# Moving the first group's DMA traffic between issuing queues, and two routers by half a product, in a Winograd-form adapter FFN

## The chip, the core and the metric

The kernel runs on one core of a Trainium2 chip. The core has a matrix engine (PE, TensorE), a vector engine (DVE, VectorE), a scalar engine (ACT, ScalarE), a general engine (POOL, GpSimd) and a synchronization engine (SP, SyncE). PE, DVE, ACT and POOL compute; SP, ACT and POOL also issue DMAs, each from its own in-order instruction queue, and all DMAs run on the same 16 DMA engines. The metric is the device time of one execution in microseconds, the median of several runs; lower is better.

## The reference, cut to what matters

```python
W = weights[condition]                        # 64 samples, each a 64x64 matrix
y = einsum('bct,bcd->bdt', x, W)              # x: 64 x 64 x 1024
xf = y.reshape(-1, 1024)                      # 4096 rows
scores = xf @ Wr.T                            # Wr: 64 x 1024
top_vals, top_idx = top_k(scores, 16)
gates = softmax(top_vals)                     # scattered into G, 4096 x 64
h = einsum('nd,krd->nkr', xf, A)              # A: 64 x 16 x 1024
out = einsum('nkr,kdr->nd', h * G[:, :, None], B)   # B: 64 x 1024 x 16
return x + out * 2.0
```

So there are two products of a 4096 x 1024 matrix with a 1024 x 1024 matrix (A and B), a small matrix per sample, and a router that scales the middle result by 64 gates per row. All arithmetic is in fp32.

## The kernel before, in words

The 4096 rows are worked in eight groups of 512 rows (`g` from 0 to 7; "group 2" is `g = 1`, "group 8" is `g = 7`). The per-sample matrix is applied after the product with A and not before it: `z = x A` first (with the router's 64 columns appended, 16 to each block of 256), then `gated` multiplies by the gathered per-sample matrices on PE and by the gates on DVE, and writes the four quarters of h into the tiles `hb`. Then follows the product with B, and the residual x is added.

Both large products are written in the Strassen-Winograd form: seven products of half-size blocks in place of eight, with sums of blocks before and after. In groups 2 to 8 this is done on two levels, so that each of the seven products (a "parent") is itself made of seven small products ("leaves"). In group 1 there is one level only, with whole blocks of A or B (`whole_parent`), and beside it DVE makes the leaf operands that all later groups need: for each of the seven first-level blocks of A (kind `h`) and B (kind `o`), differences of its quarters (`leaf_steps`). Each is written to a staging tile `staged` from the pool `bsum` (four buffers, used in turn) and stored to a scratch tensor in DRAM (`leaf_d`). Leaves that are plain quarters of a block that was itself computed (`raw`, three per block, for the four blocks p5, p6, p7, p4 of B) are stored without a step on DVE. In the trace, `hs_p_p` and `os_p_p` are the staging tiles of A and B, `h_p_p` and `o_p_p` their scratch tensors, and `lh_p_p`, `lo_p_p` the leaves fetched back (`fetch`, L458) into a ring of 13 tiles.

The order of work is written by hand. Parents run in the order h of group 1, o of group 1, h of group 2, h of group 3, o of group 2, and so on. Each parent has four lists of hooks: "mid" (after its first half), "late", "end" (after its second half), and a call `at(n, when, f)` hangs `f` on parent `n`. A hook runs in program order on whatever engine and queue its instructions belong to. The instructions of one engine are not reordered: if DVE waits for a buffer, all that stands behind it on DVE waits too, and the same is true of the DMA queues of SP, ACT and POOL.

Names and lines that matter below:

- L110 to L124: the first loads. x block 00 and the small `cond_b` go through ACT's queue; the other x blocks, the blocks of A, `wr_sb` (router weights) and the blocks of B through SP's.
- L183: `st`, the router's score product of group 1 (x with `wr_sb`), between the second and third product.
- L417: the store of a staged leaf; L411: the three `raw` stores; SP issues both, ACT the stores of the first six leaves (`apart`).
- L90 and L87 are the helpers `sub` and `add` on DVE; every sum has one of these lines.
- L489 `prepare`: four DVE sums that make the left leaf operands `l_t` of the next parent; without them the third small product of that parent can't start. It is called in the middle of the parent before.
- `a_sums`, `b_sums`: the first-level block sums; `b_sums 4` makes the block b21 that the product p4 of B uses (L542 `o_w<-b,hb`).
- L542: PE products of group 1. L505: the small products of groups 2 to 8. L556, L598, L605: copies out of PSUM on ACT.
- L161: `gather`, four indirect DMAs on POOL for each group's per-sample matrices.
- The router of groups 2 to 8: `scores`, `route_top`, `exps` (ACT), `rest` (DVE, one call for each of four tiles), `scaled` (four ACT instructions, L292), `gates` (PE transposes and an ACT copy), `gated`. In groups 2 and 8 (`near`) these stand closer together, since the next parents are already the o parents that use them.
- L741: the store of a quarter of the output, on SP; L735: the load of the residual x.

Of the kernel before, what the change touches and what calls it, by code (L numbers as in the profile page):

```python
# [9 lines left out]
F32 = mybir.dt.float32  # L10
# [5 lines left out]
P = 128  # L16
BANK = 512
# [4 lines left out]
CH = 4  # L22
HN = TPG * P // 2
HALF = BANK // 2
# [5 lines left out]
def kernel(  # L30
# [26 lines left out]
    nc = tc.nc  # L57
# [4 lines left out]
    K = wr_t.shape[1]  # L62
    NT = N // P
    NG = NT // TPG
# [19 lines left out]
    epool = early.enter_context(tc.tile_pool(name="epool", bufs=1, side="right"))  # L84
# [4 lines left out]
    def sub(o, a, b):  # L89
        nc.vector.tensor_tensor(o, a, b, ALU.subtract)  # L90
# [4 lines left out]
    def load_x(g: int, i: int, j: int, queue=nc.sync, parts=1):  # L95

        t = xq[g, i, j] = xp.tile([P, CH, HN], F32, tag=f"x{i}{j}", name=f"x_{g}_{i}{j}")
        for k in range(parts):
            s = ts(k, CH // parts)
            queue.dma_start(t[:, s, :], x_t[g, i, j][:, s, :])  # L100

    def load_block(name, src, r, c, pool, parts=1):
        t = pool.tile(src.shape[2:], F32, name=name)
        for k in range(parts):
            s = ts(k, CH // parts)
            nc.sync.dma_start(t[:, s, :], src[r, c][:, s, :])
        return t

    cond_b = const.tile([P, B], I32)
    load_x(0, 0, 0, nc.scalar, 2)  # L110
    a11 = load_block("a11", a_t, 0, 0, apool, 4)
    nc.scalar.dma_start(cond_b, cond.to_broadcast([P, B]))
    load_x(0, 1, 0)
    a21 = load_block("a21", a_t, 1, 0, apool)
    load_x(0, 0, 1)
    load_x(0, 1, 1)
    a12 = load_block("a12", a_t, 0, 1, apool)
    wr_sb = epool.tile([P, 2 * CH, K], F32, name="wr_sb")
    nc.sync.dma_start(wr_sb, wr_t.rearrange("(c p) k -> p c k", p=P))
    a22 = load_block("a22", a_t, 1, 1, apool)  # L120
    b12 = load_block("b12", b_t, 0, 1, bpool)
    b22 = load_block("b22", b_t, 1, 1, bpool)
    b11 = load_block("b11", b_t, 0, 0, epool)
    b21 = load_block("b21", b_t, 1, 0, bpool)  # L124


    row_i = const.tile([P, 1], I32)
# [29 lines left out]
    def gather(g: int):  # L157
        w_st = small.tile([P, TPG, D], F32, tag="w_st", name=f"w_st_{g}")
        for i in range(TPG):
            n = g * TPG + i  # L160
            nc.gpsimd.indirect_dma_start(  # L161
                out=w_st[:, i, :],
                out_offset=None,
                in_=cw,
                in_offset=bass.IndirectOffsetOnAxis(ap=idx[:, n : n + 1], axis=0),
            )
# [206 lines left out]
    RAW = ("p1", "p2", "p3")  # L373
# [8 lines left out]
    WIDTH = {"h": HALF + KC, "o": HALF}  # L382

    def quads(t, w):

        return [[t[:, 2 * i : 2 * i + 2, ts(j, w)] for j in range(2)] for i in range(2)]

    leaf_d = {}
# [5 lines left out]
    for j, (r, c) in {"p1": (0, 0), "p2": (1, 0), "p3": (1, 1)}.items():  # L394
        (q11, _), (q21, q22) = quads(b_t[r, c], HALF)
        leaf_d.update({("o", j, "p1"): q11, ("o", j, "p2"): q21, ("o", j, "p3"): q22})

    def leaf_steps(k, j, block, apart=None):


        (q11, q12), (q21, q22) = quads(block, WIDTH[k])
        made = {}
        queue = nc.sync if apart is None else nc.scalar

        def staged(name):
            t = bsum.tile([P, 2 * (HALF + KC)], F32, tag="leaf", name=name)
            return t[:, : 2 * WIDTH[k]].rearrange("p (c k) -> p c k", c=2)

        def raw():
            for t, p in ((q11, "p1"), (q21, "p2"), (q22, "p3")):  # L410
                nc.sync.dma_start(leaf_d[k, j, p], t)  # L411

        def step(op_, p, a, b):
            def f():
                made[p] = staged(f"{k}s_{j}_{p}")
                op_(made[p], *(made[v] if isinstance(v, str) else v for v in (a, b)))
                queue.dma_start(leaf_d[k, j, p], made[p])  # L417

            return f

        if k == "o":
            steps = [
                step(sub, "p5", q12, q11),
                step(sub, "p6", q22, "p5"),
                step(sub, "p4", q21, "p6"),
                step(sub, "p7", q22, q12),
            ]
            return steps if j in RAW else [raw] + steps
        stay.update({(k, j, "p1"): q11, (k, j, "p2"): q21, (k, j, "p3"): q22, (k, j, "p5"): q12})
        t1 = q12 if apart is None else apart.rearrange("p (c k) -> p c k", c=2)  # L430
        steps = [
            step(sub, "p7", q22, q12),
            lambda: sub(t1, q12, q11),
            step(sub, "p6", q22, t1),
            step(sub, "p4", q21, "p6"),
        ]
        return steps if apart is None else steps + [lambda: nc.scalar.copy(q12, t1)]


    parents, to_fetch, ring, stay, fetched = [], [], [], {}, [0]  # L440
# [297 lines left out]
            )  # L738

    def store(st, i, j):  # L740
        nc.sync.dma_start(  # L741
            out[ds((st["g"] * TPG + 2 * i) * P, 2 * P), ts(j, BANK)].rearrange(
                "(s p) t -> p s t", p=P
            ),
            st["os"][i, j],
        )
# [71 lines left out]
    at3 = apool.tile([P, CH, 2 * (HALF + KC)], F32, name="at3")  # L818
    at4 = apool.tile([P, CH, 2 * (HALF + KC)], F32, name="at4")
    ar = {"p1": a11, "p2": a21, "p3": a22, "p4": at4, "p5": a12, "p6": at2, "p7": at3}  # L820
    bt2 = bpool.tile([P, CH, BANK], F32, name="bt2")
    bt3 = epool.tile([P, CH, BANK], F32, name="bt3")
    br = {"p1": b11, "p2": b21, "p3": b22, "p4": b21, "p5": b12, "p6": bt2, "p7": bt3}

    sts = [{"g": g} for g in range(NG)]
    for k, g in (
# [4 lines left out]
        st = sts[g]  # L831
# [20 lines left out]
    def sums(st, which, *steps):  # L852
        for s in steps:
            st[which][s]()
# [56 lines left out]
    st = sts[0]  # L911
    h, o = st["h"], st["o"]
    steps_of(first_steps["p1"], 4)
    rows_to_gather()
    gather(0)
    steps_of(first_steps["p2"], 4)
    x_operands(st)
    sums(st, "x_sums", "s1_s2")
    a_sums(1)
# [28 lines left out]
    for k, lst, n in (  # L948
        (h + 2, b_steps, 4),
        (h + 3, b_steps, 4),  # L950
        (h + 5, a_steps, 4),
        (h + 6, a_steps, 5),
        (o, a_steps, 2),
        (o + 1, b_steps, 5),
        (o + 1, a_steps, 1),
        (o + 2, a_steps, 6),
        (o + 3, a_steps, 2),
        (o + 4, b_steps, 7),
        (o + 5, b_steps, 7),
    ):  # L960
        at(k, "end", steps_of, lst, n)
    at(o + 6, "mid", steps_of, b_steps, 2)
    at(o + 6, "end", steps_of, b_steps, 99)
    at(h + 1, "mid", gather, 1)
    for i, j in ((0, 0), (1, 0), (0, 1), (1, 1)):
        at(o, "end", load_x, 1, i, j)
    at(o + 4, "end", second_level)
    at(o + 5, "mid", fetches, 3)
    at(o + 5, "end", fetches, 3)
    h = sts[1]["h"]  # L970
# [4 lines left out]

    for st in sts[1:]:
        n, g = st["h"] + 7, st["g"]
        near = g in (1, NG - 1)
        at(n + 1, "mid", scores, st)
        at(n + 1, "late", route_top, st)  # L980
        at(n + 2, "mid", exps, st, 0, 1)
        at(n + 2, "end", exps, st, 2, 3)
        if near:
            slots = ((2, "end"), (3, "late"), (3, "end"), (4, "late"))
            pairs = {
                1: (((5, "end"), (0, 0), (1, 1)), ((6, "mid"), (1, 0), (0, 1))),
                NG - 1: (((5, "end"), (0, 0), (1, 0)), ((7, "mid"), (1, 1), (0, 1))),
            }[g]
        else:
            slots = ((3, "end"), (5, "end"), (6, "end"), (7, "late"))  # L990
            pairs = (((8, "end"), (0, 0), (1, 0)), ((9, "mid"), (1, 1), (0, 1)))
        for i, (k, when) in enumerate(slots):
            at(n + k, when, rest, st, i)
        at(n + (4 if near else 8), "end" if near else "mid", scaled, st)
        at(n + (5 if near else 8), "mid" if near else "late", gates, st)
        for (k, when), *quarters in pairs:
            for i, j in quarters:
                at(n + k, when, gated, st, i, j)
# [3 lines left out]
    for st in sts:  # L1002
        g, h, o = st["g"], st["h"], st["o"]
# [72 lines left out]
```

## Time and profile before

| | us |
|---|---|
| median of 3 runs | 801.13 (800.57 to 802.12) |
| the profiled execution | 801.74 |
| its span in the profile | 799.7 |
| PE busy | 773.6 |
| DVE busy | 623.9 |
| POOL busy | 36.5 |
| mean granted TensorE clock | 0.991 of full speed |

The span is the time from the first to the last recorded instruction; 2.0 us of the execution lie around it. PE is busy for 97% of the span, so it is idle for 26.1 us. These are spread unequally: the page's second part cuts the span into 40 slices of 20 us, and the row PE shows less than "9" in the first two slices, in the seventh (120 to 140 us, "5"), and in the last. The seventh is also the only inner slice in which the row PEclk falls. The row DMA is high in the first two slices, low from 40 to 80 us, and high again from 80 us on.

How to read it: a row of the timeline gives start and duration in us, engine, line, operation, output and inputs, and in brackets how long the engine was idle before it and who released it. A matmul of group 1 is 128x512 and takes 0.43 us start to start; a parent of group 1 takes 6.9 us.

### The profile page before, as it was taken

What the parts mean: (1) busy time and instruction counts of PE and PEld (TensorE: products, weight loads), DVE (VectorE), ACT (ScalarE), POOL (GpSimd) and SP (SyncE); (2) the same over time, 40 slices, a digit from 0 to 9 for tenths busy, and PEclk for the clock granted to TensorE, in tenths of its full rate; (3) what the DMA queues carried; (4) which work ended last, traced back from release to release, by engine and by line L of the source; (5) the groups of instructions that cost most, each with busy time, mean ns of one, the idle gap of its engine ahead of it and who ended that gap; (6) DMA issues with size and microseconds to landing.
All of it is one profiled execution on the core that took longest, in us unless ns stands there. A gap on an engine that the chain in (4) does not pass through costs nothing.

```text
span 799.7 us, 14643 instructions
## 1 busy us (share of the span) xinstructions
PE 773.6 (97%) x5342; PEld 612.2 (77%) x5342; DVE 623.9 (78%) x1310; ACT 184.1 (23%) x490; POOL 36.5 (5%) x39
## 2 busy tenths in 40 slices
PE   8899995999999999999999999999999999999996
PEld 4444444888788888888888888888788888887885
DVE  2887575677888976888778977889768888688986
ACT  0230001222222222222222222222222231232221
POOL 2200200000020020000200002000100000000000
PEclk9999997999999999999999999999999999999998
DMA  8922779764879948889488977889588894687995
GB/s 326 400 109 99 257 255 372 255 213 119 301 219 291 333 132 310 282 271 343 140 315 274 304 246 251 273 282 322 166 302 251 279 351 124 223 263 243 355 379 203
DMA packets 114982, 208.49 MB, mean 261 GB/s; under 512 B 12256, under 2 KB 31456, under 8 KB 114016
## 3 DMA queue, kind: packets, MB, share of 16 engines
q1 hardware_dynamic: 112448, 204.02, 75.3%
q10 hardware_dynamic: 1440, 2.49, 0.8%
q0 software_dynamic: 1024, 1.05, 0.5%
q8 instruction: 43, 0.70, 0.3%
q14 instruction: 27, 0.22, 0.1%
HBM read 174.41 MB, written 33.11 MB: 260 GB/s over the span
## 4 chain that ended last, share of the span: by engine, by line
PE 89%; DMA 4%; DVE 4%; issue 2%; SPq 0%; ACT 0%; DVEq 0%; ACTq 0%
PE h_p_x L505 23%; PE o_p_x L505 20%; PE h_p_w L505 11%; PE o_p_w L505 10%; PE h_p_y L505 6%; PE o_p_y L505 5%; PE zp L324 4%; PE h_x L542 3%; DMA x<-in_x_t_dram 2%; PE h_w L542 2%; PE o_x L542 2%; PE o_w L542 1%; DVE o L87 1%; DMA o_p_p<-os_p_p 1%; DMA wr_sb<-in_wr_t_dram 1%
## 5 line engine op out<-in xcount | busy, mean ns | idle before, releaser
L505 PE MATMUL o_p_x<-lo_p_p,l_t 128*128 128x256 f32 x584 | 143.3, 379 | 1.9 <-ACT l_r L598 1.8
L505 PEld LDWEIGHTS o_p_x<-lo_p_p,l_t 128*128 128x128 f32 x584 | 110.9, 190 | 17.8 <-ACT l_r L598 2.2
L87 DVE TENSOR_TENSOR o<-o,m_o_p 128x1024 f32<-128x1024 f32 (+1 forms) x67 | 78.7, 1193 | 0.5
L87 DVE TENSOR_TENSOR m_h_p<-h_p_w,l_a 128x272 f32<-128x272 f32 x49 | 21.5, 439 | 62.9 <-PE h_p_w L505 62.9
L505 PE MATMUL h_p_x<-lh_p_p,l_t 128*128 128x272 f32 x196 | 54.1, 399 | 9.3 <-issue 8.8
L87 DVE TENSOR_TENSOR m_h_p<-m_h_p,m_h_p 128x1088 f32<-128x1088 f32 x49 | 62.3, 1283 | 0.2
L505 PE MATMUL h_p_x<-a,l_t 128*128 128x272 f32 x224 | 61.4, 397 | 0.0
L161 POOL DMA_INDIRECT w_st<-in_cw_dram,idx x32 | 35.7, 1116 | 543.8 <-PE zp L324 523.6
L505 PE MATMUL h_p_w<-lh_p_p,l_t 128*128 128x272 f32 x196 | 54.6, 402 | 0.0
L505 PEld LDWEIGHTS h_p_x<-lh_p_p,l_t 128*128 128x128 f32 x196 | 37.6, 193 | 17.7 <-issue 9.2
L505 PE MATMUL o_p_w<-lo_p_p,l_t 128*128 128x256 f32 x196 | 51.0, 383 | 0.0
L505 PEld LDWEIGHTS h_p_x<-a,l_t 128*128 128x128 f32 x224 | 43.1, 193 | 8.9
L337 DVE TENSOR_TENSOR hb<-zp,gg 128x512 f32<-128x512 f32 x64 | 40.0, 683 | 10.8 <-PE zp L324 10.8
L598 ACT COPY l_b<-h_p_x 128x272 f32<-128x272 f32 x49 | 18.9, 385 | 121.9 <-PE h_p_x L505 121.9
L505 PE MATMUL h_p_x<-at,l_t 128*128 128x272 f32 x168 | 45.4, 392 | 0.0
L505 PEld LDWEIGHTS h_p_w<-lh_p_p,l_t 128*128 128x128 f32 x196 | 37.1, 194 | 7.3
L598 ACT COPY l_b<-o_p_x 128x256 f32<-128x256 f32 x49 | 18.2, 372 | 103.2 <-PE o_p_x L505 103.2
L505 PEld LDWEIGHTS o_p_w<-lo_p_p,l_t 128*128 128x128 f32 x196 | 36.6, 190 | 5.1
L87 DVE TENSOR_TENSOR m_o_p<-o_p_w,l_a 128x256 f32<-128x256 f32 x48 | 20.3, 422 | 23.7 <-PE o_p_w L505 23.7
L324 PEld LDWEIGHTS zp<-w_st,m_h_p 64*64 64x64 f32 x2048 | 31.7, 135 | 8.4 <-issue 8.4
L505 PEld LDWEIGHTS h_p_x<-at,l_t 128*128 128x128 f32 x168 | 31.9, 190 | 6.6
L324 PE MATMUL zp<-w_st,m_h_p 64*64 64x64 f32 x2048 | 34.3, 220 | 0.8 <-issue 0.8
(162 smaller groups left out, 1329.6 us busy)
## 6 DMA issues: line engine op xcount, KB each, us to landing
lo_p_p<-o_p_p SPq DMA_DIRECT2D x280, 256.0 KB, 3.9
lh_p_p<-h_p_p SPq DMA_DIRECT2D x147, 272.0 KB, 5.5
o<-in_x_dram SPq DMA_DIRECT2D x32, 512.0 KB, 7.0
lo_p_p<-in_b_t_dram SPq DMA_DIRECT2D x63, 256.0 KB, 4.4
x<-in_x_t_dram SPq DMA_DIRECT2D x31, 512.0 KB, 5.0
out_dram<-o SPq DMA_DIRECT2D x31, 512.0 KB, 5.6
o_p_p<-os_p_p SPq DMA_DIRECT2D x28, 256.0 KB, 2.9
b<-in_b_t_dram SPq DMA_DIRECT2D x4, 1024.0 KB
```

Source lines behind the costliest of these rows:

```text
L87: nc.vector.tensor_tensor(o, a, b, ALU.add)
L161: nc.gpsimd.indirect_dma_start(out=w_st[:, i, :], out_offset=None, in_=cw, in_offset=bass.IndirectOffsetOnAxis(ap=idx[:, n : n + 1], axis=0),)
L324: nc.tensor.matmul(zp[b][e * D : (e + 1) * D, c, s, :], lhsT=halves(z)[r, s, c // 2, ds(c % 2 * P + e * D, D)], rhs=ws[g][r, 2 * i + s, :] ...
L337: nc.vector.tensor_tensor(tokens(hb[j, i])[:, :, :, b, :], zp[b], g_ij[:, :, :, b, :], ALU.mult)
L505: nc.tensor.matmul(bank, lhsT=v[:, c, :], rhs=w[:, c, :width], start=first and c == 0, stop=c == 1, skip_group_check=True,)
L542: nc.tensor.matmul(piles[n, s], lhsT=left()[j][:, c, ts(s, P)], rhs=w, start=c == 0 and PILES[kind][j].isupper(), stop=c == CH - 1, skip_g ...
L598: nc.scalar.copy(par["val"][n], par["bank"]["x"])
```

## The change

The edit moves DMA issues between queues, moves some of them in time, and moves hooks. No arithmetic is added or removed.

1. First loads: a11 comes in two parts and not four; x blocks 10 and 01 and `wr_sb` go through ACT's queue and not SP's; the four blocks of B are loaded only after the first leaf stores stand in SP's queue.
2. The first six leaves (`apart`) are stored through SP's queue and not ACT's, and four of them are staged in the four `hb` tiles, which are empty until the first `gated`.
3. All other leaf stores of A and B go through POOL's queue and not SP's. The `raw` stores leave the list of steps, go through POOL's queue too, and hang on parents of their own (`raw_leaves`), three of the four blocks earlier than before.
4. The stores of group 1's output quarters go through POOL's queue.
5. The four loads of group 2's x, which stood together behind the first o parent, are spread over the next four parents. The numbers of leaf steps for each parent change with the removed `raw` steps.
6. In groups 2 and 8, the second pair of `exps`, the four `rest`, `scaled`, `gates` and the first `gated` pair each stand half a product earlier. The other groups keep their places.

```diff
     load_x(0, 0, 0, nc.scalar, 2)
-    a11 = load_block("a11", a_t, 0, 0, apool, 4)
+    a11 = load_block("a11", a_t, 0, 0, apool, 2)
     nc.scalar.dma_start(cond_b, cond.to_broadcast([P, B]))
-    load_x(0, 1, 0)
+    load_x(0, 1, 0, nc.scalar)
     a21 = load_block("a21", a_t, 1, 0, apool)
-    load_x(0, 0, 1)
+    load_x(0, 0, 1, nc.scalar)
     load_x(0, 1, 1)
+    wr_sb = epool.tile([P, 2 * CH, K], F32, name="wr_sb")
+    nc.scalar.dma_start(wr_sb, wr_t.rearrange("(c p) k -> p c k", p=P))
     a12 = load_block("a12", a_t, 0, 1, apool)
-    wr_sb = epool.tile([P, 2 * CH, K], F32, name="wr_sb")
-    nc.sync.dma_start(wr_sb, wr_t.rearrange("(c p) k -> p c k", p=P))
     a22 = load_block("a22", a_t, 1, 1, apool)
-    b12 = load_block("b12", b_t, 0, 1, bpool)
...
@@ leaf_steps
+    unused = list(hb.values())
+
     def leaf_steps(k, j, block, apart=None):
...
-        queue = nc.sync if apart is None else nc.scalar
+        queue = nc.gpsimd if apart is None else nc.sync
         def staged(name):
+            if apart is not None and unused:
+                t = unused.pop().rearrange("p c k -> p (c k)")
+                return t[:, : 2 * WIDTH[k]].rearrange("p (c k) -> p c k", c=2)
             t = bsum.tile([P, 2 * (HALF + KC)], F32, tag="leaf", name=name)
...
-        def raw():
-            for t, p in ((q11, "p1"), (q21, "p2"), (q22, "p3")):
-                nc.sync.dma_start(leaf_d[k, j, p], t)
...
+    def raw_leaves(j, block):
+        (q11, _), (q21, q22) = quads(block, HALF)
+        for t, p in ((q11, "p1"), (q21, "p2"), (q22, "p3")):
+            nc.gpsimd.dma_start(leaf_d["o", j, p], t)
...
     def store(st, i, j):
-        nc.sync.dma_start(
+        (nc.sync if st["g"] else nc.gpsimd).dma_start(
...
     steps_of(first_steps["p2"], 4)
+    for t, r, c in ((b12, 0, 1), (b22, 1, 1), (b11, 0, 0), (b21, 1, 0)):
+        nc.sync.dma_start(t, b_t[r, c])
...
         (o, a_steps, 2),
-        (o + 1, b_steps, 5),
-        (o + 1, a_steps, 1),
-        (o + 2, a_steps, 6),
+        (o + 1, b_steps, 4),
+        (o + 1, a_steps, 2),
+        (o + 2, a_steps, 5),
         (o + 3, a_steps, 2),
-        (o + 4, b_steps, 7),
-        (o + 5, b_steps, 7),
+        (o + 4, b_steps, 6),
+        (o + 5, b_steps, 6),
...
-    for i, j in ((0, 0), (1, 0), (0, 1), (1, 1)):
-        at(o, "end", load_x, 1, i, j)
+    for k, (i, j) in enumerate(((0, 0), (1, 0), (0, 1), (1, 1))):
+        at(o + 1 + k, "mid", load_x, 1, i, j)
+    for n, when, j in ((h + 5, "mid", "p5"), (h + 6, "mid", "p6"), (o, "mid", "p7"), (o + 4, "mid", "p4")):
+        at(n, when, raw_leaves, j, br[j])
...
@@ router, groups 2 and 8 (the other groups as before)
-        at(n + 2, "end", exps, st, 2, 3)
+        at(n + 2, "mid" if g in (1, NG - 1) else "end", exps, st, 2, 3)
-            slots = ((2, "end"), (3, "late"), (3, "end"), (4, "late"))
-                1: (((5, "end"), (0, 0), (1, 1)), ((6, "mid"), (1, 0), (0, 1))),
-                NG - 1: (((5, "end"), (0, 0), (1, 0)), ((7, "mid"), (1, 1), (0, 1))),
+                ((2, "late"), (2, "end"), (3, "late"), (3, "end")),
+                (4, "mid"),
+                (4, "end"),
+                ((5, "mid"), (0, 0), (1, 1) if k == 1 else (1, 0)),
+                ((6, "mid"), (1, 0), (0, 1)) if k == 1 else ((7, "mid"), (1, 1), (0, 1)),
...
-        at(n + (4 if near else 8), "end" if near else "mid", scaled, st)
-        at(n + (5 if near else 8), "mid" if near else "late", gates, st)
+        at(n + scale[0], scale[1], scaled, st)
+        at(n + turned[0], turned[1], gates, st)
```

More of the change, by code (lines that the diff above doesn't have):

```diff
@@ L110 @@
     load_x(0, 0, 0, nc.scalar, 2)
-    a11 = load_block("a11", a_t, 0, 0, apool, 4)
+    a11 = load_block("a11", a_t, 0, 0, apool, 2)
     nc.scalar.dma_start(cond_b, cond.to_broadcast([P, B]))
-    load_x(0, 1, 0)
+    load_x(0, 1, 0, nc.scalar)
     a21 = load_block("a21", a_t, 1, 0, apool)
-    load_x(0, 0, 1)
+    load_x(0, 0, 1, nc.scalar)
     load_x(0, 1, 1)
+    wr_sb = epool.tile([P, 2 * CH, K], F32, name="wr_sb")
+    nc.scalar.dma_start(wr_sb, wr_t.rearrange("(c p) k -> p c k", p=P))
     a12 = load_block("a12", a_t, 0, 1, apool)
-    wr_sb = epool.tile([P, 2 * CH, K], F32, name="wr_sb")
-    nc.sync.dma_start(wr_sb, wr_t.rearrange("(c p) k -> p c k", p=P))
     a22 = load_block("a22", a_t, 1, 1, apool)
-    b12 = load_block("b12", b_t, 0, 1, bpool)
-    b22 = load_block("b22", b_t, 1, 1, bpool)
-    b11 = load_block("b11", b_t, 0, 0, epool)
-    b21 = load_block("b21", b_t, 1, 0, bpool)
     row_i = const.tile([P, 1], I32)
@@ L421, in leaf_steps @@
         if k == "o":
-            steps = [
+            return [
                 step(sub, "p5", q12, q11),
@@ L427, in leaf_steps @@
             ]
-            return steps if j in RAW else [raw] + steps
         stay.update({(k, j, "p1"): q11, (k, j, "p2"): q21, (k, j, "p3"): q22, (k, j, "p5"): q12})
@@ L820 @@
     ar = {"p1": a11, "p2": a21, "p3": a22, "p4": at4, "p5": a12, "p6": at2, "p7": at3}
+    b12, b22, b11, b21 = (
+        (epool if n == "b11" else bpool).tile([P, CH, BANK], F32, name=n)
+        for n in ("b12", "b22", "b11", "b21")
+    )
     bt2 = bpool.tile([P, CH, BANK], F32, name="bt2")
@@ L977 @@
         n, g = st["h"] + 7, st["g"]
-        near = g in (1, NG - 1)
         at(n + 1, "mid", scores, st)
@@ L981 @@
         at(n + 2, "mid", exps, st, 0, 1)
-        at(n + 2, "end", exps, st, 2, 3)
-        if near:
-            slots = ((2, "end"), (3, "late"), (3, "end"), (4, "late"))
-            pairs = {
-                1: (((5, "end"), (0, 0), (1, 1)), ((6, "mid"), (1, 0), (0, 1))),
-                NG - 1: (((5, "end"), (0, 0), (1, 0)), ((7, "mid"), (1, 1), (0, 1))),
[L988 to L991, printed above, removed]
+        at(n + 2, "mid" if g in (1, NG - 1) else "end", exps, st, 2, 3)
+        slots, scale, turned, *pairs = {
+            k: (
+                ((2, "late"), (2, "end"), (3, "late"), (3, "end")),
[3 more added lines that the diff above has]
+                ((6, "mid"), (1, 0), (0, 1)) if k == 1 else ((7, "mid"), (1, 1), (0, 1)),
+            )
+            for k in (1, NG - 1)
+        }.get(
+            g,
+            (
+                ((3, "end"), (5, "end"), (6, "end"), (7, "late")),
+                (8, "mid"),
+                (8, "late"),
+                ((8, "end"), (0, 0), (1, 0)),
+                ((9, "mid"), (1, 1), (0, 1)),
+            ),
+        )
         for i, (k, when) in enumerate(slots):
             at(n + k, when, rest, st, i)
-        at(n + (4 if near else 8), "end" if near else "mid", scaled, st)
-        at(n + (5 if near else 8), "mid" if near else "late", gates, st)
+        at(n + scale[0], scale[1], scaled, st)
+        at(n + turned[0], turned[1], gates, st)
         for (k, when), *quarters in pairs:
```

## The prediction, made before the changed kernel was run

> **What bounds the kernel now.** I read the page first: PE is busy 97% of the span, so only PE's gaps and PE's clock can give time back. Its slices show one inner hole, the seventh (120 to 140 us):
>
> ```profile
> PE   8899995999999999999999999999999999999996
> ...
> PEclk9999997999999999999999999999999999999998
> ```
>
> Then who PE waited for (total, times, longest in us), and PE's timeline around the hole:
>
> ```profile
> PE st L183 <- DMA wr_sb<-in_wr_t_dram: 2.7, 1, 2.7
> PE o_p_x L505 <- ACT l_r L598: 1.8, 1, 1.8
> ```
>
> ```profile
> 105.16 7.13 PE L542 MATMUL o_w<-b,hb 128*128 128x512 f32 x16 [1.07 <-DVE b L90]
> ...
> 129.83 2.15 PE L505 MATMUL h_p_x<-lh_p_p,l_t 128*128 128x272 f32 x4 [8.84 <-issue]
> 131.78 2.02 PE L505 MATMUL h_p_w<-lh_p_p,l_t 128*128 128x272 f32 x4
> ```
>
> One large gap, 8.84 us from 120.99, stands between group 1 and group 2; small ones are 2.7 (router weights), 1.07 (block b21), 1.83 (group 8, at 733.3) and 0.46 (group 2, at 210.9). After the large one PE is also slow: windows of 2 us show the clock at 1.00 until 124, 0.94 in 124 to 126, 0.50 from 126 to 136. So the clock fell about 4.7 us after PE stopped, and the sixteen small matmuls from 129.83 to 136.62 took 6.79 us where 4 x 0.92 = 3.67 is usual: 3.1 us more.
>
> Why the gap? The first leaf product of group 2 needs `l_t`, which DVE makes last in this queue:
>
> ```profile
> 92.55 0.69 DVE L90 TENSOR_TENSOR os_p_p<-bt 128x512 f32<-128x512 f32 x1 [9.06 <-DMA o_p_p<-os_p_p]
> ...
> 124.96 0.69 DVE L90 TENSOR_TENSOR os_p_p<-bt,os_p_p 128x512 f32<-128x512 f32 x1 [7.18 <-DMA o_p_p<-os_p_p]
> ...
> 128.25 0.69 DVE L90 TENSOR_TENSOR os_p_p<-b 128x512 f32<-128x512 f32 x1 [0.80 <-DMA o_p_p<-os_p_p]
> 128.85 0.42 DVE L87 TENSOR_TENSOR l_t<-x 128x256 f32<-128x256 f32 x1
> 129.31 0.42 DVE L90 TENSOR_TENSOR l_t<-l_t,x 128x256 f32<-128x256 f32 x1
> ```
>
> PE restarts at 129.83, 0.1 us after the second `l_t` sum. DVE was late because a staging buffer came free late: between 83.5 and 129 it waited 9.06 + 0.86 + 1.36 + 7.18 + 0.80 = 19.3 us for leaf stores to land. SP's queue shows why:
>
> ```profile
> 79.55 1.85 SPq L100 DMA_DIRECT2D x<-in_x_t_dram  x4
> 81.45 2.59 SPq L411 DMA_DIRECT2D o_p_p<-bt  x3
> 84.14 9.45 SPq L417 DMA_DIRECT2D o_p_p<-os_p_p  x4
> ```
>
> The store issued at 84.14 has 4 x 512 KB of x and 3 x 256 KB of raw leaves before it, 2.9 MB; at the 293 to 394 GB/s of 80 to 90 us that is about 8 us, and the chain gives it 8.39.
>
> **The change, step by step.**
>
> *First loads.* The wait of 2.7 us goes if `wr_sb` lands by 21.5. Before, it was issued at 15.93, as the last of some 5.6 MB; now it stands on ACT's queue behind x, about 4.5 MB into the stream. At 326 GB/s (mean of the first 20 us) that is 14 us plus a landing of some 3. Next in line is a12's difference on DVE, which ended at 25.9, after `st`'s new end of 25.2; but it follows six leaf steps that waited 2.41 + 1.50 us for buffers, and four stages in `hb` take that away. So 2.7 is gained. Against it: a11 in halves makes the first matmul wait for 544 KB and not 272, up to 1.4 us late, with the 1.0 us wait before the second product (14.42) and a lull of the DMA at 6 to 8 us (146 GB/s) to absorb it: 0, between +1 and -1. ACT's queue is free for its first copy only after its DMAs, as now (its first work is at 21.5).
>
> *b21.* The 1.07 goes with the 9.06 us stall ahead of it on DVE. PE then arrives at the hand-over at 120.99 - 2.7 - 1.07 = **117.2**.
>
> *Leaf and output stores on POOL.* 15 + 28 leaf stores, 12 raw and 4 outputs move there, 59 DMAs. No row shows a plain DMA issued by POOL. The nearest is the gather, 128 rows by the same engine:
>
> ```profile
> 80.19 0.94 POOL L161 DMA_INDIRECT w_st<-in_cw_dram,idx  x1 [53.52 <-PE zp L324]
> 81.43 1.43 POOL L161 DMA_INDIRECT w_st<-in_cw_dram,idx  x1 [0.30 <-issue]
> ```
>
> Undisturbed, start to start is 0.94 + 0.30 = 1.25 us, and it lands 2.8 after its issue; I take 3.0 for 256 KB. A leaf store has 128 rows of 2 KB: 1.25. A raw store has 256 pieces of 1 KB, an output 256 rows. Their cost lies between 1.25 (fixed) and 2.2 (0.94 doubled, plus 0.30); SP's own issues are 0.32 for leaf and 0.5 to 1.2 for raw, so pieces do count: I take 1.5.
>
> Now the hand-over. DVE's last A step ended at 106.5; less 9.06, less 2.7, 94.7. The add for quarter 00 then waits for PE's p2 (97.1 - 2.7 = 94.4) and takes 1.28: 96.0, and I add 1.0 for buffer waits behind POOL before it: 97. From there POOL issues one output, three raw (p4), ten leaf stores and one more output before the buffer of the 14th leaf step comes free: 10 x 1.25 + 5 x 1.5 = 20.0, so 117.0; the last lands 1.75 after its issue ends, 118.75; the 14th step 0.69 and two `l_t` sums 0.88 follow: PE restarts at about **120.4**. It stands for 3.2 us, less than the 4.7 after which the clock fell, so the 3.1 us go as well. Gain: 129.83 - 120.4 = 9.4 (which holds the 2.7 and 1.07), plus 3.1.
>
> What else is queued on POOL: group 3's gather now runs behind all stores, at some 122 and not 80, and its matrices are first used in group 3's `scores` after 220: free. Output stores wait for DVE's adds, and leaf stores behind them for DVE too, in DVE's own order: no new cross wait. Raw blocks p5, p6, p7 (nine DMAs, 13.5 us) go at 50 to 76, where the DMA engines are busy 0.26 to 0.29 of the time; POOL has there about 3 + 3 DMAs in each 6.9 us product, 8.3 us, a backlog which the four-deep ring and the lighter parents that follow (2 to 4 stores each) take. SP is left with x, residual and fetches, which no longer wait behind DVE's stages; the x loads now spread over four parents.
>
> A rule speaks against this: the Trainium skill, "SBUF — State Buffer" (section "SBUF: two separate sides"), says that POOL can't write descriptors while DVE holds the shared port pair, in a two-port performance mode, or with two SBUF inputs, but then only against a POOL operation that reads SBUF. The trace shows such a block: the gather at 81.43 ends at 82.86, 0.82 after the DVE difference that ran from 81.36 to 82.04; the one at 80.19, beside a product with one PSUM input, took 0.94. The four gathers from 80.19 to 84.61 have a mean spacing of 1.47. By that row, 15 x 0.22 = 3.3 us come on top: 123.7. By the rule, the gather is blocked because it reads its indices from SBUF, a plain store reads nothing through POOL, and fp32 sums here run at 1216 ns for 1024 elements, no doubled rate: nothing comes on top. I take the rule's reading and keep 123.7 in the range.
>
> A second one: "DMA: Bandwidth & Descriptors" ("Issuing engines are not separate DMA queues") says that spreading issues saves only the sequencer's time. By it, the queue swap alone is worth SP's 0.32 us an issue, and the 9.06 would stay. The rows side with it in part: 8.39 us was mostly 2.9 MB ahead. What removes it is that x and raw move away; without those moves I would count the swap at nothing.
>
> *Router of groups 2 and 8.* At 731.72 ACT ran the four scalings (1.28 us) after waiting 2.42 for `invs`, and the copy `l_r` that PE needed stood behind them: 1.83. At 209.32 the same, 0.46. Half a product later in the new order, ACT has 1.9 to 2.4 us idle before `l_b`, and `rest` is done before: both go, 2.3. If DVE, 82 to 90% busy there, is still late, 0 to 1 stays.
>
> **Sum.** 9.4 + 3.1 + 2.3 = 14.8. Profiled execution 801.74 - 14.8 = 786.9; against the median, 0.6 lower: **786.3**.
>
> **Rivals.**
> *POOL issues faster, no gap left.* If a store costs 1.0 or less, the sum is 97 + 15 + 2 + 1.6 = 115.6, before PE's 117.2. All goes: 12.6 + 3.1 + 2.3 = 18.0, median **783.1**. For it: a store needs no index read. Against: pieces doubled.
> *Partial.* 2.2 for the 256-piece DMAs, or the port block: restart at 124, idle 6.8, clock falls again. 5.8 + 2.3 = 8.1: **793.0**. For it: raw on SP cost two to three times a leaf.
> *Slower: POOL's descriptor work becomes the bound.* Place: the 15 DMAs before `l_t`. Break-even is a restart at 129.83 + 2.3 = 132.1, so (132.1 - 97 - 1.75 - 1.6) / 15 = 2.1 us a DMA. At 1.6 for leaves and 2.55 for doubles (rows with a block of 0.35 each) the 15 take 28.8, and POOL, with six to seven DMAs a product from 54 on, starts some 5 late: 134, 1.9 slower net: **803.0**. For it: the 3.17 us gather at 23.49 beside a long difference. Against: the next at 84.61, DVE idle, is 0.94 again.
>
> **Chances.** Forecast (783.5 to 790) 0.45; no gap 0.15; partial (790 to 801) 0.25; slower 0.15. Under 0.2% (1.6 us) a measurement can't tell; some of the partial case falls there. Faster 0.80, same 0.06, slower 0.14. The range runs from 781.5 (no gap plus a better start) to 798.
>
> **What would show it.** POOL rows of the stores: near 1.25 and 1.5 us apart. `st` at about 21.5; no wait on `b`; the PE gap before the first `lh_p_p` product 0 to 4.7 us with PEclk at 9; no wait of PE on `l_r`. It is wrong if DVE's waits for stores in 95 to 120 us exceed some 12 us in all, or if a new wait stands between 25 and 97 us, where PE has none now.

## The result, and the profile after

| | before | after |
|---|---|---|
| median, us | 801.62 (800.57 to 803.27) | 796.31 (795.84 to 796.48) |
| the profiled execution, us | 801.74 | 795.84 |
| its span, us | 799.7 | 794.1 |
| PE busy, us | 773.6 | 775.3 |
| POOL busy, us | 36.5 | 69.9 |
| mean granted TensorE clock | 0.991 | 0.994 |

The ratio of the times is 0.9931, with an interval of 0.9912 to 0.9950. So the change makes the kernel faster, by some 5.5 us and not by the 14.8 forecast. The page of the changed kernel, its rows of 40 slices:

```profile
PE   8899997999999999999999999999999999999996
...
PEclk9999998999999999999999999999999999999999
```

The seventh slice has gone from 5 to 7: the hole has become smaller, it has not gone. Whom PE waited for in the changed kernel (total, times, longest, in us):

```profile
PE h_p_x L506 <- issue: 4.4, 1, 4.4
PE st L179 <- DMA wr_sb<-in_wr_t_dram: 3.2, 1, 3.2
...
PE gp L300 <- ACT g L288: 1.3, 2, 1.2
```

and where these stand in PE's timeline:

```profile
24.77 3.67 PE L179 MATMUL st<-x,wr_sb 128*64 128x256 f32 x32 [3.24 <-DMA wr_sb<-in_wr_t_dram]
...
55.54 1.21 PE L300 MATMUL gp<-ident,g 128*128 128x128 f32 x4 [1.16 <-ACT g L288]
...
126.55 2.15 PE L506 MATMUL h_p_x<-lh_p_p,l_t 128*128 128x272 f32 x4 [4.45 <-issue]
128.50 2.02 PE L506 MATMUL h_p_w<-lh_p_p,l_t 128*128 128x272 f32 x4
```

Three things are to be read here. The gap ahead of group 2 is halved, from 8.84 to 4.45. The wait for the router's weights, which was to go, has grown from 2.70 to 3.24. A wait for `g` stands at 55 us, where PE had none of that size before; the transposes `gp` that follow also take 1.21, where the kernel before had them in 0.60:

```profile
53.70 0.60 PE L304 MATMUL gp<-ident,g 128*128 128x128 f32 x4
```

The waits for b21 and for `l_r` are no longer in the list.

Read from PE's timeline, the forecast and what came compare like this:

| part, us | forecast | measured |
|---|---|---|
| PE arrives at the hand-over (before: 120.99) | 117.2: -3.8 | 122.11: +1.1 |
| gap there (before: 8.84) | 3.2: -5.6 | 4.45: -4.4 |
| first four groups of small products (before: 129.83 to 136.62, 6.79) | -3.1 | 126.55 to 133.25, 6.70: -0.1 |
| from there to the end (before: 663.1) | -2.3 | 660.85: -2.2 |
| sum | -14.8 | -5.6 |

Half of the shortfall (4.9 of 9.2) is in PE's arrival, a third (3.0) in the clock, the rest (1.2) in the gap.

**Why `wr_sb` came late.** The issue, on ACT's queue of the changed kernel:

```profile
5.44 0.39 ACTq L118 DMA_DIRECT2D wr_sb<-in_wr_t_dram  x1
```

It was issued at 5.44, ten us earlier than before, and 256 KB took 19 us to land. The trace's records of DMA packets say why. Packets that started from each queue in stretches of 2 us (those of 4 bytes are left out):

```
us from start     SP's queue             ACT's queue
 8 to 10           58 packets, 496 KB     71 packets,  18 KB   (256-byte rows: cond_b)
14 to 16           66 packets, 574 KB     68 packets, 279 KB   (4096-byte rows: x)
18 to 20           81 packets, 672 KB     87 packets,  22 KB   (256-byte rows: wr_sb)
20 to 22          279 packets, 614 KB    323 packets,  83 KB   (wr_sb)
```

The two queues pass nearly equal numbers of packets, whatever a packet's size. `wr_sb` is 1024 rows of 256 bytes; beside 8.7 KB rows on SP's queue (18 to 20 us) it gets some 3% of the bytes.

**Who else waited for it.** SP's queue of the changed kernel between 10 and 30 us, first by what its issues waited for, then in order of time:

```profile
SPq L414 <- DMA wr_sb<-in_wr_t_dram: 6.1, 1, 6.1
```

```profile
24.79 0.80 SPq L414 DMA_DIRECT2D h_p_p<-hs_p_p  x2
25.64 1.95 SPq L923 DMA_DIRECT2D b<-in_b_t_dram  x4
...
29.36 32.47 SPq L100 DMA_DIRECT2D x<-in_x_t_dram  x4
```

A leaf store, which uses nothing of `wr_sb` and whose data DVE had made by 14.9, stood in SP's queue until `wr_sb` had landed, and the four blocks of B behind it. They were issued at 25.64 (before: from 20.70). Behind them group 2's x goes out from 29.36 on (the four starts: 29.36, 41.91, 50.98, 61.50), long before the parents on which its loads hang: SP no longer waits for DVE's stages; its x issues wait only until PE and DVE have done with the old x (29.6 us in all between 28 and 66), and nothing holds them to their hooks. DVE's timeline of the changed kernel shows what follows:

```profile
37.26 0.69 DVE L90 TENSOR_TENSOR os_p_p<-b 128x512 f32<-128x512 f32 x1 [4.47 <-DMA b<-in_b_t_dram]
...
45.63 0.69 DVE L90 TENSOR_TENSOR os_p_p<-b 128x512 f32<-128x512 f32 x1 [3.79 <-DMA o_p_p<-os_p_p]
...
99.71 2.29 DVE L90 TENSOR_TENSOR b<-b,bt 128x2048 f32<-128x2048 f32 x1 [1.66 <-PE o_y L543]
...
104.51 0.68 DVE L90 TENSOR_TENSOR os_p_p<-b 128x512 f32<-128x512 f32 x1
...
112.57 0.69 DVE L90 TENSOR_TENSOR os_p_p<-b 128x512 f32<-128x512 f32 x1 [5.32 <-DMA o_p_p<-os_p_p]
...
121.84 0.69 DVE L90 TENSOR_TENSOR os_p_p<-bt,os_p_p 128x512 f32<-128x512 f32 x1 [1.85 <-DMA o_p_p<-os_p_p]
...
126.03 0.42 DVE L90 TENSOR_TENSOR l_t<-l_t,x 128x256 f32<-128x256 f32 x1
```

The waits of 4.47 and 3.79 stand in the stretch of group 1's router, which ends in `g`, for which PE waits at 55.54. The later lines are the hand-over: a wait of 1.66 of the block sum b21 for PE, which the prediction hadn't seen; waits for stores of 9.4 us in all after 106; and `l_t`, after which PE restarts at once, as before.

### The profile page after: what moved, and what is told of

Read it like the earlier page. It is cut to its first block, busy times and chain, and to the rows that moved or that the text cites. A ratio compares the mean times of both kernels' runs of the same rounds, so it can differ in the third digit from the quotient of the medians.

```text
span 794.1 us, 14663 instructions
## 1 busy us (share of the span) xinstructions
PE 775.3 (98%) x5342; PEld 612.9 (77%) x5342; DVE 623.9 (79%) x1310; ACT 184.7 (23%) x490; POOL 69.9 (9%) x98
## 4 chain that ended last, share of the span: by engine, by line
PE 89%; issue 3%; DVE 3%; DMA 2%; POOL 1%; ACT 0%; ACTq 0%; DVEq 0%; POOLq 0%
PE h_p_x L506 23%; PE o_p_x L506 20%; PE h_p_w L506 12%; PE o_p_w L506 10%; PE h_p_y L506 6%; PE o_p_y L506 5%; PE zp L320 4%; PE o_x L543 3%; PE o_w L543 2%; DMA cond_b<-in_cond_dram 1%; POOL w_st L157 1%; DMA o_p_p<-os_p_p 1%; PE gp L300 1%; DVE o L87 1%; PE sw L220 1%
## 5 line engine op out<-in xcount | busy, mean ns | idle before, releaser
L87 DVE TENSOR_TENSOR m_h_p<-h_p_w,l_a 128x272 f32<-128x272 f32 x49 | 21.5, 439 | 62.6 <-PE h_p_w L506 62.6
L606 ACT COPY m_h_p<-h_p_x 128x272 f32<-128x272 f32 x49 | 18.9, 386 | 70.7 <-PE h_p_x L506 69.2
```

Of the source, the lines that this page charges most:

```text
L87: nc.vector.tensor_tensor(o, a, b, ALU.add)
L606: nc.scalar.copy(before["q"][0][1], before["bank"]["x"])
```

## The experiments

Three questions: what the late router weights cost, what POOL's queue is worth, and what sets the gap that remains. Each ratio is to the kernel before, run beside it.

**The router weights on the other queue.** One word changes against the changed kernel:

```diff
-    nc.scalar.dma_start(wr_sb, wr_t.rearrange("(c p) k -> p c k", p=P))
+    nc.sync.dma_start(wr_sb, wr_t.rearrange("(c p) k -> p c k", p=P))
```

> The changed kernel, with wr_sb loaded through SP's queue behind x block 11 instead of ACT's queue. Theory A (wr_sb's 256-byte rows get almost no share beside SP's rows of 4 to 8 KB, and its late landing also holds SP's next issues): st starts near 21.5 us and not 24.8, the B blocks are issued near 20 and not 25.6, the 1.2 us wait before gp goes, PE reaches the hand-over near 118 and not 122.1; the time falls by 3 to 6 us from 796.3. Rival B (the DMA engines are simply full and the place in the byte stream decides): st starts at 24 or later, and the time stays within 1 us of 796.3.

Measured: 792.28 (791.95 to 793.30), ratio 0.9887 (0.9868 to 0.9906). PE's timeline, and SP's queue, of this kernel:

```profile
20.84 3.67 PE L179 MATMUL st<-x,wr_sb 128*64 128x256 f32 x32
...
123.09 2.15 PE L506 MATMUL h_p_x<-lh_p_p,l_t 128*128 128x272 f32 x4 [4.39 <-issue]
```

```profile
5.72 0.43 SPq L118 DMA_DIRECT2D wr_sb<-in_wr_t_dram  x1
...
15.74 0.86 SPq L414 DMA_DIRECT2D h_p_p<-hs_p_p  x2
19.15 4.75 SPq L923 DMA_DIRECT2D b<-in_b_t_dram  x4
```

On SP's queue 916 of the 1024 packets pass between 14 and 16 us: ACT's x blocks are through by 14.5, and no other queue takes turns with them. In the microsecond before, when both were busy, they passed 96 and 91 packets, 32 KB and 373 KB. The wait of `st` has gone, the leaf stores are issued nine us earlier, the blocks of B six and a half. PE restarts 3.5 us earlier. The wait for `g` remained (1.7), so the late issue of B's blocks alone is not what makes it.

**The router weights in long rows.** They stay on ACT's queue, but come as one row of 2 KB for each partition, laid out so by the host's setup of the inputs:

```diff
-    K = wr_t.shape[1]
+    K = wr_t.shape[2]
...
-    nc.scalar.dma_start(wr_sb, wr_t.rearrange("(c p) k -> p c k", p=P))
+    nc.scalar.dma_start(wr_sb, wr_t)
...
-        "wr_t": np.asarray(L0_ffn_Wr).T,
+        "wr_t": np.asarray(L0_ffn_Wr).T.reshape(2 * CH, P, -1).transpose(1, 0, 2),
```

> The changed kernel, wr_sb still on ACT's queue at the same place, but laid out in DRAM so that each partition's row is one piece of 2 KB and not eight of 256 bytes. Theory A (row length): wr_sb lands before 17 us, st starts near 21.5, the same 3 to 6 us faster than 796.3 as with the queue moved. Rival C (ACT's queue is served after SP's, whatever its rows): wr_sb lands after 23, no change, 796.3.

Measured: 791.97 (790.83 to 792.39), ratio 0.9875 (0.9856 to 0.9894). `st` starts at 21.60 with no wait. The packets share as before (18 to 20 us: 68 and 69, 592 KB against 141 KB, now 2048 bytes each). It did not land before 17 as expected but at about 21.5, since x stands before it. By the difference to the changed kernel's median, the late `wr_sb` cost 4.0 to 4.3 us. The gap at the hand-over is the same again: 4.44.

**Stores back on SP's queue.** The change with the `nc.gpsimd` of the leaf, raw and output stores put back to `nc.sync`, every hook left where the change has it:

```diff
-        queue = nc.gpsimd if apart is None else nc.sync
+        queue = nc.sync
...
-            nc.gpsimd.dma_start(leaf_d["o", j, p], t)
+            nc.sync.dma_start(leaf_d["o", j, p], t)
...
-        (nc.sync if st["g"] else nc.gpsimd).dma_start(
+        nc.sync.dma_start(
```

> The changed kernel with all leaf, raw and output stores of group 1 back on SP's queue, at the changed kernel's places; everything else as changed. The prediction's reading (the queue itself saves only issue time; what moved is x and raw): within 2 us of 796.3. Rival (POOL's queue brings the hand-over's gain): the hand-over restarts near 130 again, and the time returns to 799 or more. What could make it faster than 796.3: leaf stores stand behind fewer loads, since SP waits for DVE's stages before it issues x.

> The kernel with wr_sb in long rows, and the leaf, raw and output stores of group 1 back on SP's queue at the changed places. What POOL's queue is worth was 1.8 us with the late wr_sb. If it is the hand-over's landing alone: again 1.5 to 3 us, 793.5 to 795. If POOL's queue was worth little because of the early stores' collision with x: 4 us or more, 796. If the queue is worth nothing by itself: 792.

Measured for the first: 798.11 (796.20 to 798.50), ratio 0.9949 (0.9931 to 0.9968). PE's waits in it:

```profile
PE h_p_x L506 <- issue: 6.8, 1, 6.8
PE st L179 <- DMA wr_sb<-in_wr_t_dram: 2.6, 1, 2.6
```

The second is the same edit made on the kernel with long rows: 793.63 (792.30 to 794.30), ratio 0.9903 (0.9880 to 0.9925), gap 6.82. So by the medians POOL's queue is worth 1.8 us with the weights late (798.11 - 796.31) and 1.7 with them in time (793.63 - 791.97). The intervals of either pair overlap, so the times alone don't show it; that the gap is 2.4 longer without it, in both traces, does. In the first of these two traces `st` also ran at half clock (5.31 us for 3.67), which the second has not. The rest of the old wait of 9.06 went with the x loads and the earlier raw stores: DVE waited for B's leaf stores 19.3 us between 80 and 129 in the kernel before, and 13.8 in this one. In neither of the two kernels does PE wait over 0.2 for `g`: with stores among them on SP's queue, x no longer runs ahead. (The first is a weak witness, since the slow `st` also made PE later.)

**The router part alone.** The kernel before with only the hooks of groups 2 and 8 moved (point 6 of the change).

> The kernel before with the router places of groups 2 and 8 alone changed. If the two waits on the copy l_r (0.46 and 1.83 us) go and nothing takes their place: 2.0 to 2.3 us faster than before. Rival (they come back as waits for gp or DVE): less than 1 us faster.

Measured: 800.37 (797.60 to 801.61), ratio 0.9978 (0.9967 to 0.9989): 1.9 us by the medians, 0.9 to 2.6 by the interval. The waits of PE for `l_r` are gone, and the gap stands as before (8.84).

**What sets the gap.** In three kernels that reach the hand-over at 122.1, 118.7 and 118.5, the gap was 4.45, 4.39 and 4.44. It must hang on something that moves along with PE. DVE's timeline of the kernel with long rows:

```profile
96.07 2.29 DVE L90 TENSOR_TENSOR b<-b,bt 128x2048 f32<-128x2048 f32 x1 [1.81 <-PE o_y L543]
...
100.87 0.68 DVE L90 TENSOR_TENSOR os_p_p<-b 128x512 f32<-128x512 f32 x1
...
108.97 0.69 DVE L90 TENSOR_TENSOR os_p_p<-b 128x512 f32<-128x512 f32 x1 [5.36 <-DMA o_p_p<-os_p_p]
...
118.20 0.69 DVE L90 TENSOR_TENSOR os_p_p<-bt,os_p_p 128x512 f32<-128x512 f32 x1 [1.84 <-DMA o_p_p<-os_p_p]
...
121.93 0.42 DVE L87 TENSOR_TENSOR l_t<-x 128x256 f32<-128x256 f32 x1
```

PE ends the product p2 at 95.87 here and at 99.51 in the changed kernel. From there it is 5.0 to the first step of B in both, then 22.04 to the restart in both, and 22.60 to PE's arrival in both; 27.04 - 22.60 = 4.44. The sum b21 overwrites a block that p2 reads, so DVE's queue to `l_t` starts from PE's p2, and PE gaining time ahead of p2 can't close the gap. What stands between the two ends can: fewer leaf steps, less traffic ahead of the stores. Four edits of that kernel, each by itself:

```diff
@@ two leaf steps after the first l_t and not ahead of it
-    at(o + 6, "mid", steps_of, b_steps, 2)
@@ raw stores of p4 after the leaves (part of the line)
-                    (o + 4, "mid", "p4")):
+                    (o + 6, "end", "p4")):
@@ x of group 2 issued by ACT, so that it keeps to its hooks
-        at(o + 1 + k, "mid", load_x, 1, i, j)
+        at(o + 1 + k, "mid", load_x, 1, i, j, nc.scalar)
@@ six leaf steps after the first l_t
-        (o + 4, b_steps, 6),
-        (o + 5, b_steps, 6),
+        (o + 4, b_steps, 4),
+        (o + 5, b_steps, 4),
-    at(o + 6, "mid", steps_of, b_steps, 2)
```

> The kernel with wr_sb in long rows (792.0), and the two B steps that stand ahead of prepare in the last o parent moved behind it. If DVE's queue ahead of l_t sets the restart: the restart comes 1.3 us sooner, the gap is 3.1 and not 4.4, and if the clock then does not fall some 3 us more: 787.5 to 790.7. If the fetched leaf or a DMA sets it: no change, 792.

> The kernel with wr_sb in long rows, and the three raw stores of p4 hung on the end of the last o parent and not before the B steps. If the landing of the first B stores behind 768 KB of raw pieces is what DVE waits 5.4 us for: that wait falls by about 2 us and the restart comes up to 2 us sooner: 787 to 790. If only DVE's and PE's own order counts (quarter p4 done, 1.8 us wait later): no change, 792.

> The kernel with wr_sb in long rows, and the four x loads of group 2 issued from ACT's queue at the same hooks, so that they can't run ahead to 29 us as they do on SP. If they crowd the first B stores (landing 5 to 8 us at 36 to 46): DVE's waits there shrink and the 0.7 us wait before gp goes: 790.5 to 791.5. Rival (the B blocks and the residual do it): 792. If x then collides with the stores after 80 us: slower, 792 to 794.

> The kernel with wr_sb in long rows, and six B steps moved from ahead of prepare to behind it (4, 4 and 0 ahead and 8 behind, in place of 6, 6, 2 and 2). If the steps before l_t are the gap: PE's gap goes to 0 to 1 us, the clock stays, 784 to 787. If the eight steps behind hold DVE up in group 2's first products instead: PE waits there for l_t or l_r, and the time is 788 to 793.

| edit | median, us | ratio | gap, PE restarts |
|---|---|---|---|
| none (long rows) | 791.97 | 0.9875 (0.9856 to 0.9894) | 4.44, 122.91 |
| two steps later | 790.17 | 0.9863 (0.9837 to 0.9889) | 3.71, 122.33 |
| raw later | 790.62 | 0.9857 (0.9832 to 0.9882) | 3.55, 121.94 |
| x by ACT | 791.65 | 0.9878 (0.9854 to 0.9902) | 5.52, 122.89 |
| six steps later | 787.91 | 0.9829 (0.9805 to 0.9853) | none there; 2.24, 126.39 |

The first three lie within each other's intervals and that of the kernel they start from: only their traces tell them apart. With the raw stores later, the wait of 5.36 for the first leaf store fell to 1.73, but later waits for stores grew, and PE restarted only 1.0 sooner. With x held to its hooks, PE reached the hand-over 1.1 us sooner: the wait for `g` fell from 0.70 to 0.2, and `gp` got shorter (x now leaves from 71.86 on, and not into B's first stores). The restart stayed where it was. The first step of B came 5.0 after p2's end here too, so 1.1 sooner (99.77), but from there to the restart it was 23.12 and not 22.04: with x among the later stores, DVE waited 0.81 and 0.76 for stores of A's leaves, where it had no such wait before:

```profile
99.77 0.68 DVE L90 TENSOR_TENSOR os_p_p<-b 128x512 f32<-128x512 f32 x1
...
101.99 0.69 DVE L90 TENSOR_TENSOR os_p_p<-b,os_p_p 128x512 f32<-128x512 f32 x1 [0.81 <-DMA h_p_p<-hs_p_p]
103.44 0.69 DVE L90 TENSOR_TENSOR os_p_p<-b 128x512 f32<-128x512 f32 x1 [0.76 <-DMA h_p_p<-hs_p_p]
```

With six steps moved, the first gap is gone and another one opens a parent later, in PE's timeline of that kernel:

```profile
126.39 1.16 PE L506 MATMUL h_p_x<-lh_p_p,l_t 128*128 128x272 f32 x4 [2.24 <-issue]
127.38 1.74 PE L506 MATMUL h_p_w<-lh_p_p,x 128*128 128x272 f32 x4
```

The next parent's `l_t` now stands behind the eight steps moved.

**Steps spread, raw later.** So the steps must be spread, not pushed: on the kernel with long rows, the raw stores of p4 later and 2, 5 and 4 steps of B behind three parents, with five left for after the `l_t`. Two steps are then made two parents earlier than in the change.

```diff
+        (o + 2, b_steps, 2),
...
-        (o + 4, b_steps, 6),
-        (o + 5, b_steps, 6),
+        (o + 4, b_steps, 5),
+        (o + 5, b_steps, 4),
...
-    at(o + 6, "mid", steps_of, b_steps, 2)
...
-                    (o + 4, "mid", "p4")):
+                    (o + 6, "end", "p4")):
```

> The kernel with wr_sb in long rows; two B steps earlier (third o parent), 5 + 4 ahead of prepare and 5 behind, the raw stores of p4 at the end of the last o parent. If DVE's store waits ahead of l_t are the whole gap: PE's gap between the groups is 0 to 1 us, the second one (2.2 us with eight steps behind) 0 to 1 us, the clock stays, 784 to 787. If the DMA engines, full from 105 to 122 us, only pass the wait on to the fetches: 787 to 790.

> The same, with group 2's x loads issued from ACT's queue at their hooks. PE came 1.1 us sooner to the hand-over with this, and gained nothing since DVE's chain ended at the same time; with that chain shorter the 1.1 us count: 783 to 786. If the x loads collide with the stores of the last parents instead: no better than without, 785 to 788.

Measured: **784.78** (784.46 to 785.17), ratio 0.9794 (0.9770 to 0.9818), 2.1% faster than the kernel before and faster than the changed one. PE's timeline at the hand-over, and DVE's:

```profile
117.88 1.08 PE L506 MATMUL h_p_y<-a,x 128*128 128x272 f32 x4
118.79 1.08 PE L506 MATMUL h_p_x<-lh_p_p,l_t 128*128 128x272 f32 x4
```

```profile
113.88 0.69 DVE L90 TENSOR_TENSOR os_p_p<-bt,os_p_p 128x512 f32<-128x512 f32 x1 [3.48 <-DMA o_p_p<-os_p_p]
...
116.13 0.42 DVE L90 TENSOR_TENSOR l_t<-l_t,x 128x256 f32<-128x256 f32 x1
```

DVE still waits 3.48 us for a store, but `l_t` is ready 2.2 us before PE asks for it: the wait is off the path. There is no gap, and the granted clock stays 1.00 there. The two edits were not tried apart. The same kernel with x issued by ACT gave 785.19 (784.48 to 787.07), ratio 0.9797 (0.9773 to 0.9821): not distinguishable, with small gaps of 0.35 and 1.24 in its trace.

## Why the prediction was right and wrong, step by step

Most of the shortfall comes from three steps: where `wr_sb` lands and where the x loads go (4.9 us in PE's arrival), and when the clock falls (3.0). The mechanism of the gap held.

**Direction and mechanism of the gap: right.** A staging buffer that came free late held DVE, and `l_t` with it; moving traffic shortened DVE's waits for B's leaf stores between 80 and 129 us, from 19.3 us to 11.2, and PE's gap from 8.84 to 4.45. The time lies inside the range.

**First loads, "So 2.7 is gained": wrong, and the largest error.** The step placed `wr_sb` by how many bytes stood before it (4.5 MB at 326 GB/s). The bytes ahead didn't decide: the queues shared by packet, and 256-byte packets beside 8.7 KB ones got 3% of the bytes. In place of -2.7 came +0.5 at `st`. The two runs that mend `wr_sb` alone bring 4.0 and 4.3 us of the time.

**SP's queue, "the x loads now spread over four parents": wrong.** A hook places an issue in the program, not in time; with the stores gone from SP's queue, x ran ahead into B's first stores, DVE was late with group 1's router, and PE waited 1.16 for `g` and took 0.61 more for `gp`. The kernels that let x run ahead wait 0.6 to 1.7 (0.3 with two steps moved); those that hold it, by stores on SP's queue or by ACT, at most 0.2. The prediction had named a new wait between 25 and 97 us as a sign that it is wrong, and that sign appeared. With b21's 1.07 gone, 0.5 + 1.16 + 0.61 - 1.07 = 1.2, against the +1.1 seen in PE's arrival.

**b21: right as a wait of PE, wrong in what it starts.** The 1.07 went. But "The add for quarter 00 then waits for PE's p2" named only one tie to p2; the sum b21 itself waits for p2, and costs 2.29 after it. So the first step of B came 5.0 after p2's end and not 2.6. PE's own lateness moved both by another 5.1 (99.51 for 94.4), which the gap doesn't show.

**POOL's issues: wrong sizes that nearly cancel.** Forecast 1.25 for a leaf and 1.5 for a raw or output store. POOL's timeline in the changed kernel:

```profile
102.93 0.54 POOL L414 DMA_DIRECT2D h_p_p<-hs_p_p  x1 [7.07 <-DVE hs_p_p L90]
103.69 0.54 POOL L414 DMA_DIRECT2D h_p_p<-hs_p_p  x1 [0.22 <-issue]
104.89 0.72 POOL L742 DMA_DIRECT2D out_dram<-o  x1 [0.65 <-DVE o L87]
105.60 2.12 POOL L438 DMA_DIRECT2D o_p_p<-b  x3
107.33 2.54 POOL L414 DMA_DIRECT2D o_p_p<-os_p_p  x4
```

A leaf store takes 0.54, 0.76 start to start; the four issued in a row from 107.33 on stand some 0.53 apart, though each lasts 0.94. Raw and output stores take 0.70 to 0.72. The gather's row was a bad neighbour for them. POOL wasn't what DVE waited for: the DMA engines were full (share 0.88, 1.00 and 0.96 in the three stretches from 106 to 112), and the first leaf store after the raw ones freed its buffer only at 112.5, some five us after its issue. The run with the raw stores later shows their part: there this wait was 3.6 us shorter. The term for landing, "1.75 after its issue ends", didn't hold there. In sum 22.04 from the first step of B to the restart, forecast 23.4: right within 6%, by another cause, and so by luck. The rival "no gap" had the issue cost right, and it fell over the same DMA engines; the rival "POOL becomes the bound" is refuted by 0.54.

**The gap: 3.2 forecast, 4.45 found.** By the terms above: 2.4 more ahead of the first step (5.0 for 2.6), 1.4 less after it (22.04 for 23.4), 0.2 because PE takes 22.6 from p2 to its arrival and not 22.8.

**The port rule: read rightly.** The forecast took nothing for DVE's sums blocking POOL. Of the 28 leaf stores of B from POOL, 24 last 540 to 582 ns, whether DVE is running or not; the other four are those from 107.33 on, and DVE stood still beside them.

**Issuing queues: too low.** "Without those moves I would count the swap at nothing" was not tried as such; with the moves made, the swap of queues is worth 1.7 to 1.8 us by the medians, and 2.4 us of gap.

**The clock, "less than the 4.7 after which the clock fell": wrong rule.** Windows of 1 us of the changed kernel (PE, PEld, DVE, ACT and POOL busy, then granted clock, DMA share, GB/s):

```profile
121.00:122.00 1.00, 1.00 (x5) 0.57 (x3) 0.16 (x1) 0.39 (x1) 0.00 (x0) 1.00 1.01 397
...
125.00:126.00 1.00, 0.00 (x0) 0.00 (x0) 0.99 (x2) 0.00 (x0) 0.94 (x3) 0.86 0.60 229
126.00:127.00 1.00, 0.45 (x1) 0.48 (x2) 0.97 (x3) 0.00 (x0) 0.49 (x1) 0.50 1.01 381
```

Taking a mean of 0.86 as 0.72 us at 1.00 and the rest at 0.50, the clock fell at 125.7, 3.6 us after PE stopped. Read in the same way, it fell 4.8 us after in the kernel before, 5.3 with stores on SP's queue, and 2.1 with the weights on SP's queue. In the kernel with two steps moved it fell when PE was already at work again, 4.9 us after a stop of 3.71:

```profile
122.00:123.00 1.00, 0.67 (x3) 0.62 (x4) 1.00 (x4) 0.00 (x0) 0.44 (x1) 1.00 0.58 217
123.00:124.00 1.00, 1.00 (x5) 0.77 (x4) 0.96 (x2) 0.39 (x1) 0.20 (x1) 0.76 1.01 389
```

So the delay read from one trace is no limit below which a gap is safe. The 13 traces together show more. In each of them the moments at which the granted clock changes lie a whole multiple of 3.41 us apart: at the hand-over the clock stayed low for 3.41, 6.83 or 10.24 us. Cut at every 3.41 us on this grid, a trace falls into stretches, and the clock fell at the end of each stretch at full clock in which PE had stood idle for 1.97 us or more (26 falls), and after none with 1.92 or less. The two closest cases, from the kernel with x by ACT (busy 1.49 of 3.41, no fall at 119.29) and the one with six steps moved (busy 1.44, a fall at 127.83):

```profile
115.88:119.29 3.41, 1.49 (x7) 0.90 (x5) 1.49 (x3) 0.39 (x1) 0.79 (x3) 1.00 0.90 368
```

```profile
124.42:127.83 3.41, 1.44 (x6) 1.11 (x7) 3.20 (x8) 0.90 (x3) 2.10 (x3) 1.00 0.87 300
```

This rule is read from the traces and was not tried by a run of its own. It explains why the wait of 3.24 at `st` in the changed kernel had no fall behind it (the grid split it into 1.78 and 1.46) while the stop of 2.24 had one. By it a stop of 3.2 us escapes only where the grid splits it so that neither part reaches 1.97: by an estimate in one case of five (0.74 of 3.41 us), if the place of the grid is left to chance. So the forecast's 3.1 us would most likely have been lost in part even with the gap that it expected. The Trainium skill, "TensorE: Matmul & The Clock Gate" (section "What's actually happening"), says that the gate watches a window of some 3.4 us that runs freely, not one that begins with the gap; the grid of 3.41 us agrees.

**Router: right.** -2.3 forecast, -2.2 in the changed kernel from the fifth group of small products to the end, -1.9 by itself.

## What to carry to other kernels

Before a small load is moved to another queue, look at the length of its rows against the rows on the queues beside it, for the queues shared by packet here and not by byte, and ask what else waits for it. When a stall is removed, follow the late engine back to the last thing it takes from the engine that it keeps waiting: from there on the gap is a difference of two lengths, and gains ahead of that point don't shorten it. A stop need not last as long as the delay seen in one trace to bring the clock down: here 2 us of idle time in one stretch of the grid were enough. A hook without a wait in its queue fixes an order, not a time.

## What was not expected of the hardware

- Two busy queues shared by packet: 81 and 87 packets in 2 us, 672 KB on one and 22 KB on the other. 256 KB in 256-byte rows took 19 us.
- A store waited 6.1 us on SP for a load on ACT's queue that it doesn't use; with the weights in long rows it left at 21.62, again just after they had landed. That this is a shared completion semaphore is an inference; it was not tried by itself.
- A plain store issued by POOL mostly took 0.54 us (128 rows of 2 KB) and 0.70 to 0.72 (256 pieces of 1 KB, or 256 rows of 2 KB), against 0.94 for a gather of 128 rows, and didn't grow beside DVE's sums.
- The granted clock changed only at steps of 3.41 us, and fell after each step in which PE had been idle for 1.97 us or more, and after none with 1.92 or less; so it fell 2.1 to 5.3 us after PE had stopped at the hand-over, in two kernels after it had started again.
